# Two attention blocks: residual additions by accumulating transfers, the last pair's reciprocals spread inside VectorE, and the normed input in one ScalarE step

## The chip, the cores and the metric

The kernel runs on one core of a Trainium2 chip. The metric is the device time of that core in microseconds (us), for all eight images and both layers in one launch. A core has five engines that run their own queues in order and meet only at semaphores: TensorE (PE, matrix products), VectorE (DVE), ScalarE (ACT), GpSimd (POOL) and SyncE (SP, which here issues the transfers). Sixteen DMA engines move data between HBM and the on-chip buffer, whoever issues the transfer.

## What is computed

Eight images of 512 channels by 1024 pixels pass through two blocks of the same form: group norm, a 1x1 convolution to q, k and v, attention with 8 heads of 64 channels over the 1024 pixels, an output projection with bias, and the residual addition. Cut to what matters:

```
xg = x.reshape(B, GROUPS, -1)
xn = ((xg - mean) * rsqrt(var + EPS)).reshape(B, C, H, W)
xn = xn * norm_gamma[None, :, None, None] + norm_beta[None, :, None, None]
qkv = einsum('oc,bchw->bohw', qkv_w, xn) + qkv_b[None, :, None, None]
attn = softmax(einsum('bhds,bhdt->bhst', q, k) * scale, axis=-1)
out = einsum('bhst,bhdt->bhds', attn, v).reshape(B, C, H, W)
return x + einsum('oc,bchw->bohw', proj_w, out) + proj_b[None, :, None, None]
```

The second block has the same mathematics with separate weights wq, wk, wv, wp. Everything is float32.

## The kernel before

A job is one image in one layer: 16 jobs, numbered 0 to 15, in pairs of images (two images in layer 0, then the same two in layer 1). Two images lie in the on-chip buffer as `x` tiles of 4 channel chunks by 1024 pixels. The job's output is added into the same tile (the residual), so job n+2 reads as input what job n wrote when n is in layer 0. When n is in layer 1 the finished quarters are stored and the next image is loaded in their place.

All projections use a fast matrix-product scheme with seven products for a 2x2 block product (`ORDER`, `OUTER`, line 42 on), which trades products on TensorE for sums of blocks on VectorE. The V projection uses one level of it. The K, Q and output (O) projections use two levels: seven outer products ("chains"), each of seven inner products of 128x128 by 256 columns.

Stages, in the order in which TensorE runs them:

1. **Attention of job n** (`Attention.run`, L829): 8 groups (a pair of heads and half of the pixels) of 8 steps. In a step TensorE makes scores `sc` (L740), ScalarE makes `e = exp(sc)` (L745), VectorE adds `e` into the group's row sums `acc` (L757), and TensorE multiplies `e` with `v` into `po` (L771). At a group's end (`finish`, L776) VectorE reduces `acc` to `r` (L783) and adds the two halves of `po` into `q` (L790), which from then on holds the attention's output. After each second group four small transfers gather `r` into `lr` (L800), `invert` makes the reciprocals (L808 to L811), one transfer writes them to a DRAM scratch `rd` (L812), two transfers broadcast them from there to all partitions as `rb` (L817), and `normalise` (L823) multiplies `q` by `rb`.
2. **V phase of job n+1** (`v_phase`): 14 steps of 4 products (L443). Its results leave PSUM by ScalarE copies (L456) and VectorE additions (L458). During it VectorE makes the sums of the attention's output that the O projection needs (`out_sums`, L866: `to`, lines 337 to 343, and `os`, lines 472 to 477).
3. **Deep phases** (`deep_phases`, L512): 21 chains of 7 products (L574), O of job n, then K and Q of job n+1. Chain c+1 starts before chain c ends. Each chain fills an `epool` tile `p` with four pieces, two by ScalarE (L584, L586) and two by VectorE (L588, L590). The function `end` (L594) queues what is to be done with finished `p` tiles in a list `outer`. For O these are the residual additions, `x += p` on VectorE (`more`, L609, recorded at L603). Two of the seven products of each chain (7 and 3) take one step from the lists: `soon` (sums for later chains) and then `outer`, or, where `outer` is empty, `extra` (statistics of the next input, loads of the next image, all with a lowest chain number).

The order on each engine is written by hand. `later(delay, fn)` puts a step at a model time, `advance` moves that time while products are recorded, and `chores` puts steps at numbered steps of the attention: 64 steps in an attention. In chores lie the norm of the next input (`scale` on VectorE, L273, then `shift` on ScalarE in place, L279), its sums (L337 to L343) and, from job 3 on, half of the two-level sums (`deep_first[4:]`). The other half, and in the first jobs both, is put into the V phase and after it with `later`.

Buffers: `epool` has LEAD + 3 = 5 tiles of 4 KB per partition, shared by the `e` of the attention and the `p` of the deep phases. The weights of the chains come through a ring of RING = 8 tiles, fetched by SP 2.5 model us after a tile is used (`used`, L201). The output bias (`make_out_bias`, L906: the projection of the v bias) is made after attention 0 and attention 2 with two `epool` tiles, three loads and VectorE steps at the start of the V phase. Factors of weights for later jobs are made in the attentions 0 to 2 (`first_factors`).

Of the kernel before, what the change touches and what calls it, by code (L numbers as in the profile page):

```python
# [9 lines left out]
F32 = mybir.dt.float32  # L10
# [34 lines left out]
RING = 8  # L45
# [25 lines left out]
def fast_path(  # L71
# [13 lines left out]
    epool = ctx.enter_context(tc.tile_pool(name="epool", bufs=LEAD + 3))  # L85
# [130 lines left out]
    class Norm:  # L216


        def __init__(self, n):
            b, layer = jobs[n]  # L220
            self.n, self.b, self.layer = n, b, layer
            self.stats = small.tile([P, NC, 2, 6], F32, tag="stats", name=f"stats_{n}", bufs=1)
            self.mv = small.tile([P, NC, 2], F32, tag="mv", name=f"mv_{n}")
            self.mr = small.tile([P, NC, 2], F32, tag="mr", name=f"mr_{n}")
            self.mul = small.tile([P, NC], F32, tag="mul", name=f"mul_{n}", bufs=1)

# [39 lines left out]
        def factors(self, chunks):  # L266
            g0 = self.layer * NVEC + GAMMA
            nc.vector.tensor_mul(
                self.mul[:, chunks], self.mr[:, chunks, 1], env.vec_sb[:, g0 : g0 + NC][:, chunks]
            )  # L270

        def scale(self, cc, cols=slice(0, S)):
            nc.vector.tensor_scalar(  # L273
                xn[0][:, cc, cols], xs[self.b][:, cc, cols], self.mr[:, cc, 0:1],
                self.mul[:, cc : cc + 1], ALU.subtract, ALU.mult,
            )

        def shift(self, cc, cols=slice(0, S)):
            nc.scalar.activation(  # L279
                xn[0][:, cc, cols], xn[0][:, cc, cols], AF.Identity,  # L280
                bias=env.vec(self.layer, BETA, cc),
            )
# [24 lines left out]
    def norm_steps(n):  # L307
        norm = Norm(n)

        def scale(cc):  # L310
            if cc == 0:
                norm.factors(slice(0, NC))
                xn[0] = acts.tile([P, NC, S], F32, tag="xn", name=f"xn_{n}")
            norm.scale(cc)

        shift = norm.shift
        reads = [lambda cc=cc, sh=sh: norm.stat(cc, sh) for cc in range(NC) for sh in range(2)]
        reads.append(norm.gather)
        steps = [norm.groups]
        for cc in range(NC + 1):  # L320
            def both(cc=cc):
                if cc > 0:
                    shift(cc - 1)
                if cc < NC:
                    scale(cc)
            steps.append(both)
# [185 lines left out]
    def deep_phases(n, extra, outs=None):  # L512
# [81 lines left out]
        def end(c):  # L594
# [10 lines left out]
            if which == O:  # L605
# [3 lines left out]
                def more(oh, sh, *parts):  # L609
                    to_ = xt[:, 2 * oh : 2 * oh + 2, sh * HALF : (sh + 1) * HALF]  # L610
                    for part in parts:
                        add(to_, to_, p(part))

                def done(oh, sh):
                    if layer == 1:
                        rows = slice(oh * CH, (oh + 1) * CH)
                        cols = slice(sh * HALF, (sh + 1) * HALF)
                        last = outer.pop()
                        outer.append(lambda: (last(), nc.sync.dma_start(
                            out[b, rows, cols].rearrange("(c p) s -> p c s", p=P),  # L620
                            xt[:, 2 * oh : 2 * oh + 2, cols],
                        )))
# [3 lines left out]
                elif o == 2:  # L626
                    more(0, 0, 2)
                    done(0, 0)
                elif o == 6:
                    add(p(6), p(6), p(1))  # L630
                    more(0, 1, 6)
                elif o == 5:
                    more(0, 1, 5)
                elif o == 7:
                    add(p(7), p(7), p(6))
                    more(1, 1, 7, 5)
                    done(1, 1)
                elif o == 3:
                    more(1, 0, 7)
                    more(0, 1, 3)  # L640
                    done(0, 1)
                elif o == 4:
                    more(1, 0, 4)
                    done(1, 0)
# [75 lines left out]
    class Attention:  # L720
# [55 lines left out]
        def finish(self, g):  # L776

            n, q, m = self.n, self.q, g % 2
            hp, sh = self.groups[g]
            to_ = q[:, hp, sh * HALF : (sh + 1) * HALF]  # L780
            if m == 0:
                self.r = small.tile([P, 2, RP], F32, tag="r", name=f"r_{n}_{g}", bufs=1)
            nc.vector.tensor_reduce(  # L783
                self.r[:, m, :], self.acc.pop(g).rearrange("p j (b e) -> p (j b) e", e=RP), AX.X,
# [13 lines left out]
            lr = small.tile([RP, NQ, 2, RP], F32, tag="lr", name=f"lr_{n}_{g}", bufs=1)  # L798
            for i in range(NQ):
                nc.sync.dma_start(lr[:, i], self.r[i * RP : (i + 1) * RP])  # L800
            rd = dram.tile([2, 2, HALF], F32, tag="rd", name=f"rd_{n}_{g}")
            rb = []

            def invert():
                lt = small.tile([RP, 2, RP], F32, tag="lt", name=f"lt_{n}_{g}", bufs=1)
                ri = small.tile([RP, 2, RP], F32, tag="ri", name=f"ri_{n}_{g}", bufs=1)
                rt = small.tile([RP, 2, RP], F32, tag="rt", name=f"rt_{n}_{g}", bufs=1)
                nc.vector.tensor_reduce(lt, lr.rearrange("p a g b -> p g b a"), AX.X, ALU.add)  # L808
                nc.vector.reciprocal(ri, lt)
                for i in range(2):  # L810
                    nc.vector.transpose(rt[:, i, :], ri[:, i, :])  # L811
                nc.sync.dma_start(rd.rearrange("m j (b e) -> (j b) m e", e=RP), rt)  # L812
                nc.vector.tensor_max(lmax, lmax, lt)
                nc.vector.tensor_max(rmax, rmax, ri)
                rb.append(apool.tile([P, 2, HALF], F32, tag="rb", name=f"rb_{n}_{g}", bufs=1))
                for j in range(2):
                    nc.sync.dma_start(  # L817
                        rb[0][j * HD : (j + 1) * HD],
                        rd[:, j, :].unsqueeze(0).to_broadcast([HD, 2, HALF]),
                    )  # L820

            def normalise():
                nc.vector.tensor_mul(place, place, rb[0])  # L823

            ends = g + 1 == len(self.groups)
            later(9.9 if ends else 7.6, invert)
            later(16.4 if ends else 16.2, normalise)

# [16 lines left out]
    def judge():  # L845
        nc.vector.tensor_max(lmax, lmax, rmax)
        nc.vector.tensor_max(lmax[:, 0, :], lmax[:, 0, :], lmax[:, 1, :])
        worst = small.tile([RP, RP], F32, tag="worst", name="worst", bufs=1)
        nc.vector.tensor_copy(worst, lmax[:, 0, :])
        nc.vector.tensor_reduce(worst[:, 0:1], lmax[:, 0, :], AX.X, ALU.max)  # L850
        turned = small.tile([RP, RP], F32, tag="turned", name="turned", bufs=1)
# [14 lines left out]
    def out_sums(n, outs):  # L866
# [10 lines left out]
        steps = outs.steps(0) + [start] + outs.steps(3) + outs.steps(1) + [part(1)]  # L877
        steps += outs.steps(2) + [part(2)] + outs.steps(4) + [part(3)]
        early = 9.0 if n in (0, 2) else 3.2
        times = (0.3, 1.1, 1.9, early, early + 0.8, 15.2, 16.0, 16.8, 18.0, 18.8, 19.6, 20.8, 21.6, 22.4)  # L880
# [25 lines left out]
    def make_out_bias(layer, delay):  # L906


        rows = [
            epool.tile([P, 2, HALF], F32, tag="e", name=f"rows_{layer}_{i}") for i in range(2)  # L910
        ]
        bvb = apool.tile([P, C], F32, tag="px", name=f"bvb_{layer}")
        for i in range(2):
            nc.sync.dma_start(
                rows[i], wrows[layer][i * CH : (i + 1) * CH].rearrange("(oc p) c -> p oc c", p=P)
            )
        nc.sync.dma_start(bvb, bv[layer : layer + 1, :].to_broadcast([P, C]))

        def part(oc):
# [471 lines left out]
```

## Time and profile before

| | us |
|---|---|
| median of three runs | 3327.54 |
| lowest and highest | 3326.61, 3329.2 |
| profiled execution: run, and span from the first to the last instruction | 3330.16, 3328.4 |
| attention to attention (start of the scores), jobs 5 to 6 | 1142.26 to 1345.88: 203.6 |
| the same, jobs 1 to 2 | 301.04 to 517.23: 216.2 |
| VectorE busy, ScalarE busy | 2854.9, 1893.4 |
| GpSimd busy | 24.0 |

A line of an instruction group reads: line, engine, operation, tile written and tiles read, shapes, count, then busy time and mean duration in ns, then the time that the engine sat idle just before these instructions and what ended most of it. TensorE's busy time counts overlapping matmuls, so it is not a measure of useful work; what matters are its idle times. The stage from the end of one attention to the start of the next takes about 90 us of the 203.6, the attention about 113.

### The profile page before, as it was taken

The page shows a single profiled execution, that of the slowest core. Times are in us where ns is not written, and L with a number is a line of the kernel's source. Part 1 is how long each engine was busy: PE and PEld are TensorE (multiplying, and loading weights), DVE is VectorE, ACT ScalarE, POOL GpSimd, SP SyncE. Part 2 cuts the span into 40 slices and gives each one's busy share as a digit, 9 for nine tenths or more (in the row PEclk, how much of TensorE's full clock was granted, in tenths as well). Part 3 has the DMA queues.
Part 4 walks back from the last instruction along what each step waited for, and adds up shares of the span by engine and source line. Part 5 has one row for each costly group of instructions (what it writes and reads, how often), then busy time and mean ns, then how long its engine had stood idle before and what let it go on. Part 6 is the DMA issues. An engine that isn't in the chain of part 4 may idle for free.

```text
span 3328.4 us, 57847 instructions
## 1 busy us (share of the span) xinstructions
PE 3225.0 (97%) x22870; PEld 1854.2 (56%) x22870; DVE 2854.9 (86%) x3980; ACT 1893.4 (57%) x3026; POOL 24.0 (1%) x31
## 2 busy tenths in 40 slices
PE   9989999999999999999999999999999999999999
PEld 7356374473745737456383664836547365473743
DVE  8997988988889898888988889788897888989876
ACT  4646646456464664646646466564655646566463
POOL 0000000000000000000000000000000000000000
PEclk9999999999999999999999999999999999999999
DMA  8234142250412304124051221403315031230401
GB/s 296 69 126 115 66 140 83 68 189 15 151 59 60 100 22 121 33 71 139 22 181 30 78 76 27 135 21 103 108 37 174 15 104 56 55 106 16 144 26 47
DMA packets 143863, 289.98 MB, mean 87 GB/s; under 512 B 40040, under 2 KB 52960, under 8 KB 142560
## 3 DMA queue, kind: packets, MB, share of 16 engines
q1 hardware_dynamic: 143584, 286.22, 28.1%
q8 instruction: 181, 2.97, 0.4%
q14 instruction: 98, 0.80, 0.1%
HBM read 232.73 MB, written 51.31 MB: 85 GB/s over the span
## 4 chain that ended last, share of the span: by engine, by line
PE 72%; DVE 20%; DMA 4%; issue 2%; ACT 2%; SPq 1%; DVEq 0%; POOL 0%; ACTq 0%
PE sc L740 24%; PE po L771 22%; PE vd L574 9%; PE zd L574 8%; DVE acc L757 4%; PE yd L574 3%; PE ud L574 3%; DMA rb<-rd 2%; DVE x L603 1%; ACT e L745 1%; DVE os L472 1%; DVE v L458 1%; DVE os L473 1%; PE pp L709 1%; DVE os L476 1%
## 5 line engine op out<-in xcount | busy, mean ns | idle before, releaser
L745 ACT ACTIVATE e<-sc 128x1024 f32<-128x1024 f32 x1024 | 1043.1, 1023 | 572.9 <-PE sc L740 486.5
L740 PE MATMUL sc<-q,k 64*64 64x512 f32 x8192 | 1064.3, 591 | 20.9 <-ACT e L745 18.9
L771 PE MATMUL po<-e,v 64*64 64x512 f32 x8192 | 1058.9, 590 | 0.0
L757 DVE TENSOR_TENSOR acc<-acc,e 128x1024 f32<-128x1024 f32 x768 | 936.4, 1219 | 54.5 <-ACT e L745 6.9
L740 PEld LDWEIGHTS sc<-q,k 64*64 64x64 f32 x8192 | 308.3, 133 | 587.5 <-issue 531.1
L771 PEld LDWEIGHTS po<-e,v 64*64 64x64 f32 x8192 | 313.5, 133 | 566.4 <-issue 557.4
L574 PE MATMUL vd<-deep,w 128*128 128x256 f32 x900 | 256.6, 384 | 6.5 <-DVE p L590 6.0
L574 PE MATMUL zd<-deep,w 128*128 128x256 f32 x892 | 247.9, 380 | 0.9 <-DVE p L588 0.6
L755 DVE TENSOR_TENSOR acc<-e,e 128x1024 f32<-128x1024 f32 x128 | 156.4, 1222 | 103.0 <-ACT e L745 103.0
L574 PEld LDWEIGHTS vd<-deep,w 128*128 128x128 f32 x900 | 168.1, 190 | 49.3 <-DVE p L590 14.4
L574 PEld LDWEIGHTS zd<-deep,w 128*128 128x128 f32 x892 | 169.6, 190 | 24.5 <-DVE p L588 1.0
L603 DVE TENSOR_TENSOR x<-x,p 128x1024 f32<-128x1024 f32 x135 | 164.2, 1216 | 0.0
L783 DVE TRANSPOSE_TENSOR_REDUCE r<-acc 128x32 f32<-128x1024 f32 x128 | 158.6, 1239 | 0.6
L574 PE MATMUL vd<-os,w 128*128 128x256 f32 x420 | 126.7, 391 | 28.4 <-DVE p L588 28.4
L443 PE MATMUL z<-w,t 128*128 128x256 f32 x480 | 116.1, 391 | 24.7 <-DVE v L458 24.7
L456 ACT COPY v<-z 128x512 f32<-128x512 f32 x32 | 18.7, 586 | 180.8 <-PE z L443 180.8
L443 PEld LDWEIGHTS z<-w,t 128*128 128x128 f32 x480 | 92.8, 196 | 42.9 <-DVE v L458 30.3
L823 DVE TENSOR_TENSOR q<-q,rb 128x1024 f32<-128x1024 f32 x64 | 77.5, 1212 | 44.8 <-DMA rb<-rd 44.8
L603 DVE TENSOR_TENSOR p<-p,p 128x1024 f32<-128x1024 f32 x94 | 114.3, 1216 | 0.0
L443 PE MATMUL z<-w,xn 128*128 128x256 f32 x480 | 110.1, 383 | 0.0
L592 ACT COPY s<-zd 128x256 f32<-128x256 f32 x173 | 64.6, 373 | 77.5 <-PE zd L574 77.5
L574 PEld LDWEIGHTS vd<-os,w 128*128 128x128 f32 x420 | 79.1, 193 | 49.0 <-DVE p L588 39.2
(201 smaller groups left out, 3947.0 us busy)
## 6 DMA issues: line engine op xcount, KB each, us to landing
w<-deep SPq DMA_DIRECT2D x287, 448.0 KB
w<-keep SPq DMA_DIRECT2D x129, 256.0 KB
rb<-rd SPq DMA_DIRECT2D x128, 256.0 KB
deep<-w SPq DMA_DIRECT2D x42, 448.0 KB
x<-x_dram SPq DMA_DIRECT2D x28, 512.0 KB
out_dram<-x SPq DMA_DIRECT2D x28, 512.0 KB
keep<-raw SPq DMA_DIRECT2D x5, 1792.0 KB
lr<-r SPq DMA_DIRECT2D x256, 8.0 KB
```

The lines of the kernel that those rows point to most:

```text
L443: nc.tensor.matmul(ps[:, ti * CH : (ti + 1) * CH], r[:, cc, t0 : t0 + P], w[:, cc, :], start=(start and ti == 0 and cc == 0), stop=(cc == ...
L458: nc.vector.tensor_add(to_, tokens(ps), tokens(s5))
L574: nc.tensor.matmul(ps, lhs[:, FACTOR[i], :], moving[i], start=start, stop=True, skip_group_check=True,)
L592: return chain(product, lambda ps: nc.scalar.copy(s5, ps), put, z, y, u, w)
L603: outer.append(lambda: nc.vector.tensor_add(to_, a, b))
L740: nc.tensor.matmul(sc[h * HD : (h + 1) * HD, j, :], k[r, hp, k0 : k0 + HD], q[r, hp, sh * HALF : (sh + 1) * HALF], start=True, stop=True,)
L745: nc.scalar.activation(e, sc, AF.Exp, scale=SCALE)
L755: nc.vector.tensor_add(acc[g], self.es[i - 1], e)
L757: nc.vector.tensor_add(acc[g], acc[g], e)
L771: nc.tensor.matmul(po[g][j * HD : (j + 1) * HD, h, :], v[r, kc, d0 : d0 + HD], e[r, j, :], start=(kc == 0), stop=(kc == NT - 1),)
L783: nc.vector.tensor_reduce(self.r[:, m, :], self.acc.pop(g).rearrange("p j (b e) -> p (j b) e", e=RP), AX.X, ALU.add, apply_transpose=True,)
L823: nc.vector.tensor_mul(place, place, rb[0])
```

## The change

- **Residual additions.** `more` no longer queues a VectorE addition `x += p`. It issues a transfer on the GpSimd queue that adds `p` into the quarter of `x` (`accum_op=ALU.add`), nine per job, 512 KB each. Some are issued at the chain's end, others from the list `outer` after a VectorE sum they need. The first part of quarter (1, 0) is added at the end of outer product 7, no longer at that of outer product 3. The stores of finished quarters are put 8 model us later with `later`.
- **Last pair of an attention.** The gather of `r` becomes three VectorE copies, and the broadcast becomes three small copies and one VectorE transposition of a 128 x 1024 stretch, in place of transfers. Its steps are put at 0.0, 0.2, 2.0 and 4.0 in place of 9.9 and 16.4. The other pairs keep their way through DRAM, with three gathering transfers in place of four (the first quarter stays where it is).
- **Normed input.** `scale` and `shift` become one ScalarE step with a factor and an offset per channel, made by two more tiny VectorE operations. In the opening job two of four chunks are done by VectorE in one step.
- **Output bias.** Its loads and eight VectorE steps move from the V phase after attentions 0 and 2 to the list `extra` of the deep phases before attention 0 and before attention 2. Its buffers come from `apool`.
- **Buffers and order.** `epool` has 6 tiles and the weight ring 7. The sums for O are put earlier in the V phase. The direct two-level sums of the next input (`deep_first[:4]`) move from the V phase to `extra` in the O chains, and the others (`deep_first[4:]`) to the attention in all jobs. Statistics start at chain 15 in place of 14, loads of the next image at 11 in place of 8. The first input's statistics for job 1 move ahead of attention 0, and factors of weights start a little earlier.

The core of the diff:

```
-RING = 8
+RING = 7
...
-    epool = ctx.enter_context(tc.tile_pool(name="epool", bufs=LEAD + 3))
+    epool = ctx.enter_context(tc.tile_pool(name="epool", bufs=LEAD + 4))
...
+        def apply(self, cc, cols=slice(0, S), scalar=True):
+            to_, x, one = xn[0][:, cc, cols], xs[self.b][:, cc, cols], slice(cc, cc + 1)
+            if scalar:
+                nc.scalar.activation(
+                    to_, x, AF.Identity, bias=self.off[:, one], scale=self.mul[:, one]
+                )
...
-                def more(oh, sh, *parts):
-                    to_ = xt[:, 2 * oh : 2 * oh + 2, sh * HALF : (sh + 1) * HALF]
-                    for part in parts:
-                        add(to_, to_, p(part))
...
+                def more(oh, sh, part, ends=False):
+
+                    cols = slice(sh * HALF, (sh + 1) * HALF)
+                    to_ = xt[:, 2 * oh : 2 * oh + 2, cols]
+                    nc.gpsimd.dma_start(to_, p(part), accum_op=ALU.add)
+                    if ends and layer == 1:
                         rows = slice(oh * CH, (oh + 1) * CH)
...
+                        later(8.0, lambda: nc.sync.dma_start(
+                            out[b, rows, cols].rearrange("(c p) s -> p c s", p=P), to_
+                        ))
...
                 if o == 1:
                     more(0, 0, 1)
                 elif o == 2:
-                    more(0, 0, 2)
-                    done(0, 0)
+                    more(0, 0, 2, True)
                 elif o == 6:
                     add(p(6), p(6), p(1))
-                    more(0, 1, 6)
+                    outer.append(lambda: more(0, 1, 6))
                 elif o == 5:
-                    more(0, 1, 5)
+                    more(1, 1, 5)
+                    outer.append(lambda: more(0, 1, 5))
                 elif o == 7:
                     add(p(7), p(7), p(6))
-                    more(1, 1, 7, 5)
-                    done(1, 1)
+                    outer.append(lambda: (more(1, 1, 7, True), more(1, 0, 7)))
                 elif o == 3:
-                    more(1, 0, 7)
-                    more(0, 1, 3)
-                    done(0, 1)
+                    more(0, 1, 3, True)
                 elif o == 4:
-                    more(1, 0, 4)
-                    done(1, 0)
+                    more(1, 0, 4, True)
...
+            def spread():
+                if ends:
+                    nc.vector.transpose(
+                        box[0].rearrange("p m (b e) -> p m b e", e=RP),
+                        ri[:, :, 0, :].unsqueeze(3).to_broadcast([P, 2, RP // 2, RP]),
                     )
...
+            times = (0.0, 0.2, 2.0, 4.0) if ends else (0.0, 7.6, 7.7, 16.2)
+            for at, step in zip(times, (gather, invert, spread, normalise)):
+                later(at, step)
...
-        times = (0.3, 1.1, 1.9, early, early + 0.8, 15.2, 16.0, 16.8, 18.0, 18.8, 19.6, 20.8, 21.6, 22.4)
+        times = (0.1, 1.0, 2.5, 4.5, 5.5, 6.5, 7.5, 8.6, 14.0, 15.8, 16.5, 17.5, 19.2, 21.0)
...
-            for at, step in zip((4.8, 6.0, 8.9, 10.1, 30.0, 31.5, 33.0, 34.5), deep_first):
-                later(at, step)
...
-            extra = deque()
+            extra = deque((0, fn) for fn in deep_first[:4])
             if jobs[n][1] == 1 and jobs[n][0] + 2 < B:
-                extra.append((8, lambda b=jobs[n][0] + 2: (x_tile(b), load_x(b))))
+                extra.append((11, lambda b=jobs[n][0] + 2: (x_tile(b), load_x(b))))
...
-                extra.extend((14, fn) for fn in reads)
+                extra.extend((15, fn) for fn in reads)
```

## The prediction

> **What bounds the kernel now.** I read the page's engine line first and then the groups of TensorE with their idle times, because TensorE runs almost without a break and only its waits can be won.
>
> ```profile
> PE 3225.0 (97%) x22870; PEld 1854.2 (56%) x22870; DVE 2854.9 (86%) x3980; ACT 1893.4 (57%) x3026; POOL 24.0 (1%) x31
> ...
> L740 PE MATMUL sc<-q,k 64*64 64x512 f32 x8192 | 1064.3, 591 | 20.9 <-ACT e L745 18.9
> ...
> L574 PE MATMUL vd<-deep,w 128*128 128x256 f32 x900 | 256.6, 384 | 6.5 <-DVE p L590 6.0
> ...
> L603 DVE TENSOR_TENSOR x<-x,p 128x1024 f32<-128x1024 f32 x135 | 164.2, 1216 | 0.0
> ...
> L574 PE MATMUL vd<-os,w 128*128 128x256 f32 x420 | 126.7, 391 | 28.4 <-DVE p L588 28.4
> L443 PE MATMUL z<-w,t 128*128 128x256 f32 x480 | 116.1, 391 | 24.7 <-DVE v L458 24.7
> ...
> L823 DVE TENSOR_TENSOR q<-q,rb 128x1024 f32<-128x1024 f32 x64 | 77.5, 1212 | 44.8 <-DMA rb<-rd 44.8
> ```
>
> TensorE's own waits sum to 20.9 + 6.5 + 28.4 + 24.7 = 80.5 us, and 11.3 more before the group zd<-os (further down the list of groups): 92 us of 3328. Almost all end with VectorE (p, v) or ScalarE (e). So work taken off VectorE pays where it delays a p, v or e, and not elsewhere. Where is that? The busy times by stage of one middle job (columns: stretch, its length, busy us of PE, weight loads, DVE, ACT, POOL, granted clock, DMA share, GB/s) and the timeline of its V phase:
>
> ```profile
> 1255.30:1279.10 23.80, 22.80 (x108) 19.80 (x105) 19.34 (x32) 5.21 (x9) 0.00 (x0) 1.00 0.47 140
> 1279.10:1300.50 21.40, 19.39 (x89) 16.46 (x89) 18.46 (x35) 11.60 (x31) 0.00 (x0) 1.00 0.36 108
> 1300.50:1345.90 45.40, 45.27 (x214) 39.61 (x212) 36.11 (x58) 28.99 (x76) 0.00 (x0) 1.00 0.43 127
> 1345.90:1459.00 113.10, 112.21 (x1031) 39.79 (x1031) 101.95 (x116) 73.22 (x77) 1.40 (x1) 1.00 0.09 23
> ```
>
> ```profile
> 1274.64 1.23 DVE L823 TENSOR_TENSOR q<-q,rb 128x1024 f32<-128x1024 f32 x1 [2.71 <-DMA rb<-rd]
> ...
> 1277.32 2.00 PE L443 MATMUL z<-w,t 128*128 128x256 f32 x8 [1.00 <-DVE v L458]
> ...
> 1285.97 0.70 PE L574 MATMUL vd<-os,w 128*128 128x256 f32 x2 [1.05 <-DVE p L588]
> ```
>
> VectorE stands still for 2.71 us on the broadcast of the reciprocals, the sums of O behind it are late, and TensorE waits in the V phase and twice in the O chains (the second time at 1299.29, 0.96 us). In the K and Q chains (third row) TensorE loses nothing. The place is the O boundary.
>
> **What the Trainium skill says.** (1) "DMA: Bandwidth & Descriptors", Anatomy of one DMA: a transfer costs about 2.0 us plus its bytes at 436 GB/s, so 3.2 us for 512 KB. Here two broadcasts, 512 KB together, take 5.1 to 6.6 us in the chain of waits. So contention adds to it. (2) The same page, SWDGE vs HWDGE: accumulation goes through GpSimd alone, which makes the descriptors in software. No run here shows it yet. (3) "Collectives: The Full Stack", the bandwidth ceiling: an add in the transfer is half as fast because it reads two sources, not because adding takes time. Not shown here either. (4) "SBUF — State Buffer", Who interferes with whom: a two-input VectorE operation does not stop descriptor writing. The trace before has no such case.
>
> **The change part by part**, against the profiled span of 3328.4 (0.9 above the median run, which is less than I can resolve).
>
> *Residual additions.* 135 x 1.216 = 164.2 us leave VectorE, 10.9 per boundary, all in or just after the O chains. In return deep_first[:4], 4 x 1.22 = 4.9 us, comes from the V phase into the O chains. The second row's 18.5 us becomes about 12.5 of 21.4, and the V row loses 4.9.
>
> *Last pair.* The wait on rb<-rd (44.8 us over 14 boundaries) goes. Added per job: six small copies (no row; the 32x64 rows of L813 and L814 take 0.17 to 0.20, a 128x2 copy 0.16) about 1.0 us, and one transposition of 128x1024. No row has it: at least 0.18 (a 32x32 one, L811), at most about twice a 1024-column pass. I take 1.24, which the transposing reduction over 1024 columns takes (L783). Two 0.18 go away. Net 1.9 us more busy and about 3 less waiting, but the normalised q comes earlier: VectorE ends r 3.4 us after TensorE's last product of the attention (timeline), then copies 1.0, reduction and reciprocal 1.1, maxima 0.4, transposition 1.24, first sums 1.6, product 1.2: at about 10 us, against 20.5 now (1275.87 - 1255.4). The V phase then holds 19.3 - 4.9 + 1.9 us and O sums that were late before (about 5), so 21 of 24: no wait, and the product that waited at 1277.32 has its v about 4 us early.
>
> *Normed input.* L273 leaves (52.2 us, 3.2 per attention). ScalarE's count stays at 60 full pieces of 1.10 us, and it no longer waits for L273 (46.5 us). The attention's slip (0.68 us of idle at 1196.8, where e comes late) should mostly go. A sixth e tile helps the same.
>
> *Output bias.* Its eight steps (0.68 each, 5.5 us a time) and a 4.5 us wait for loads leave the V phases after attentions 0 and 2, where TensorE loses most (216.2 us for that job against 203.6). They come back in chains before attentions 0 and 2, with weight preparation there: I charge 3 us.
>
> *Two-level sums to the attention in jobs 0 to 2*: 3.8 us of VectorE, against 3.2 freed. Nothing, since the stage has about 11 us of slack (fourth row). Ring of 7: TensorE uses a weight tile every 7 x 0.43 = 3.0 us, so six ahead are 18 us of cover against a few us of landing: nothing. SP gains: 448 small transfers for reciprocals become 288. It gets later stores, behind which weights queue; the 18 us cover these.
>
> *Sum.* Each wait also costs the refilling: the pair after a wait takes 0.70 us for 0.43 (above), so 0.27 x about 85 waits = 23 us beside the 92. I take nearly all of z<-w,t (25 of 28), three quarters of vd<-os (27 of 36), 8 of zd<-os (the rest waits for prepared weights), 15 of 26 in the scores, nothing of vd<-deep: 75. Less 3 for the bias: 72.
>
> *What the transfers may give back.* A p tile is free only when its transfer has landed. With 0.43 us a product, counted from the start of O: the tile of chain 5 is wanted again by chain 11, whose first piece is written after 81 products, at 34.8. The quarter (0, 1) takes three transfers, each waiting for the one before. The first needs the VectorE sum after chain 2, at 24 x 0.43 + 1.2 = 11.5. So they fit if 3T < 23.3: T, from issue to landing, up to 7.8 us. My estimate of T: 2.0 + 2 x 1.2 = 4.4 us alone by (1) and (3). With 0.4 of the DMA engines taken by weights (DMA share above) the moving part stretches to 4 us, so 6.0, and about 0.5 for descriptors. Lower bound 3.2 (a plain copy), upper bound 10 to 11 if adding halves the rate again. At 6.5 it fits by 4 us, but eight transfers at 2.4 to 2.9 us of all 16 engines (19 to 23) and ten weights of 448 KB at 436 GB/s (10.5) make 30 to 34 us of work in a window of 30.5, so some chains will wait. I charge 1 us in each of 15 boundaries. 3328 - 72 + 15 = 3271; I say 3270.
>
> **The rivals.**
> 1. *Likeliest, 3270 (own range 3238 to 3300)*: as above. For it: every large wait names VectorE, and the K and Q chains show that VectorE at 80% leaves no wait.
> 2. *Half of the relief: 3308.* The waits come from bursts (two sums and an addition in one slot), not from the load. Sums for O and deep_first now share chains 0 to 3. Then z<-w,t goes (25), little else (10), less the 15. Against it: the slots that hold an addition today lose it.
> 3. *Slower: 3355 and above.* The accumulating transfer takes T = 10 us. Then quarter (0, 1) is done at 11.5 + 30 = 41.5, chain 11 waits 6.7 us behind ScalarE's first write, TensorE behind that, 15 times: 3256 + 100 = 3356. At T = 11, 3401. It decides from 11.5 + 3T = 34.8 + 72/15, T = 9.4 us. For it: no row prices accumulation, and the DMA engines already work at 0.36 to 0.47 in these stages. Against it: source (3).
> 4. *No change*: T near 9.4, between the two.
>
> That the change misses its aim is ruled out: the built order of the changed kernel has 135 transfers x<-p on GpSimd and no addition x<-x,p.
>
> **How the numbers follow.** Likeliest 0.52; half 0.18; slower 0.25; no change 0.05. A measurement of this kernel tells about 0.2%, 6.7 us, from no change: faster 0.70, same 0.05, slower 0.25. About 0.06 lies below 3236, and about 0.13 above 3360, so the range is 3236 to 3360.
>
> **What would show it.** VectorE busy near 2855 - 164 - 52 + 30 = 2670. Idle before z<-w,t under 3 us and before vd<-os under 10. The wait on rb gone at the boundaries. The groups ACT p (L584, L586 before) with no long idle ended by a DMA: if a row names the x<-p transfer there, or the statistics wait for it, rival 3 is at work. If the waits on p stay with no DMA in them, it is rival 2. A transposition far above 2.5 us would make the V phase wait again.

## The result and the profile after

The changed kernel takes 3369.55 us (median of four runs, 3366.25 to 3372.11) against 3328.37 beside it (3326.61 to 3330.59): ratio 1.0123, 95% interval 1.0105 to 1.014. It is 1.2% slower. Forecast were 3270 and a gain of 1.7%; the time lies above the range.

From the page of the changed kernel: the engine line, the DMA queue that GpSimd issues on (packets, MB, share of 16 engines' span), groups in the form explained above, and the issues of x<-p (count, size, median us from issue to landing).

```profile
PE 3248.1 (97%) x22870; PEld 1872.5 (56%) x22870; DVE 2701.4 (80%) x3895; ACT 1889.1 (56%) x3022; POOL 189.3 (6%) x166
...
q0 software_dynamic: 36720, 70.79, 12.2%
...
L723 PE MATMUL sc<-q,k 64*64 64x512 f32 x8192 | 1062.7, 590 | 4.5 <-ACT e L728 2.3
...
L565 PE MATMUL zd<-deep,w 128*128 128x256 f32 x892 | 264.5, 400 | 73.6 <-ACT yd L381 69.2
...
L565 PE MATMUL vd<-deep,w 128*128 128x256 f32 x900 | 265.1, 395 | 15.4 <-ACT yd L381 11.4
...
L565 PE MATMUL vd<-os,w 128*128 128x256 f32 x420 | 119.2, 381 | 2.0 <-DVE p L581 1.3
L434 PE MATMUL z<-w,t 128*128 128x256 f32 x480 | 111.0, 380 | 0.0
...
x<-p POOLq DMA_DIRECT2D x135, 512.0 KB, 8.5
```

Everything that the change was to relieve is relieved. The idle time before vd<-os falls from 28.4 to 2.0 us, before z<-w,t from 24.7 to 0.0, before the scores from 20.9 to 4.5. In its place stands a wait that was not there: 73.6 us before zd<-deep and 15.4 before vd<-deep, in chains where TensorE lost 7.4 us in all before (0.9 and 6.5). The engine named is ScalarE (yd), which only copies. What ScalarE itself waits for stands in the waits of the changed kernel (engine, tile and line that waited, what for, us in all, count, longest):

```profile
POOL x L604 <- DMA x<-p: 160.0, 36, 8.8
DVE p L579 <- DMA x<-p: 77.9, 17, 5.8
DVE p L581 <- DMA x<-p: 73.9, 23, 5.1
ACT p L575 <- DMA x<-p: 71.6, 26, 5.5
ACT p L577 <- DMA x<-p: 67.3, 25, 4.8
```

ScalarE stands 139 us (71.6 + 67.3) at the first piece of a `p` tile, and a transfer x<-p has not yet emptied that tile. The copies of `yd` that TensorE needs are queued behind. GpSimd stands 160 us because the transfer before it into the same quarter has not landed. One boundary shows how this comes about. It is the boundary before attention 6, called job 6 below: the O chains of job 5, which begin at 1279.5, then the K and Q chains of job 6. Selected lines from the timeline of the changed kernel (start, us, engine, line, operation, then idle time before and what ended it):

```profile
1286.44 1.20 POOL L604 DMA_DIRECT2D x<-p  x1 [117.07 <-ACT p L575]
1293.15 1.20 POOL L604 DMA_DIRECT2D x<-p  x1 [5.51 <-ACT yd L381]
...
1294.27 1.22 DVE L594 TENSOR_TENSOR p<-p,p 128x1024 f32<-128x1024 f32 x1
...
1295.79 2.43 POOL L604 DMA_DIRECT2D x<-p  x2 [1.44 <-DVE p L594]
1304.84 1.20 POOL L604 DMA_DIRECT2D x<-p  x1 [6.62 <-DMA x<-p]
1309.34 2.43 POOL L604 DMA_DIRECT2D x<-p  x2 [3.30 <-DMA x<-p]
1313.76 0.37 ACT L575 COPY p<-yd 128x256 f32<-128x256 f32 x1 [3.37 <-DMA x<-p]
1314.29 1.20 POOL L604 DMA_DIRECT2D x<-p  x1 [2.51 <-DVE p L579]
1314.46 0.70 PE L565 MATMUL zd<-deep,w 128*128 128x256 f32 x2 [2.42 <-ACT yd L381]
1320.55 0.47 ACT L577 ACTIVATE p<-yd,vec_sb 128x256 f32<-128x256 f32 x1 [4.28 <-DMA x<-p]
1321.35 1.46 PE L565 MATMUL zd<-deep,w 128*128 128x256 f32 x4 [1.91 <-ACT yd L381]
1324.22 0.37 ACT L575 COPY p<-yd 128x256 f32<-128x256 f32 x1 [0.91 <-DMA x<-p]
```

With chains counted from 0, the six `p` tiles go round, so chain 9 needs the tile of chain 3. That tile is read by two transfers, and the second of them is the second into quarter (0, 1). It could be issued only at 1304.84, when the first, issued at 1295.79, had landed (9.0 us), and landed itself at 1313.76 (8.9 us). ScalarE waits 3.37 us for it, then 4.28 for the tile of chain 4 (issued at about 1310.5, free at 1320.55: 10.0 us) and 0.91 for that of chain 5 (1314.29 to 1324.22: 9.9 us). TensorE loses 2.42 and 1.91 us. Around these two waits, in windows of the changed kernel (stretch, length, busy us of PE, weight loads, DVE, ACT, POOL, granted clock, DMA share, GB/s):

```profile
1311.80:1315.20 3.40, 0.98 (x5) 0.68 (x4) 1.42 (x2) 0.95 (x4) 0.92 (x1) 1.00 1.08 283
1315.20:1318.60 3.40, 3.40 (x9) 2.70 (x8) 0.47 (x2) 0.72 (x2) 0.28 (x1) 0.50 1.14 210
1318.60:1322.00 3.40, 1.49 (x7) 0.99 (x6) 1.44 (x2) 1.05 (x3) 0.99 (x1) 1.00 1.07 248
1322.00:1325.40 3.40, 3.40 (x10) 2.69 (x9) 0.57 (x2) 1.56 (x4) 0.21 (x1) 0.50 1.01 170
```

Two things are to be seen. The DMA share is at or above 1.0, so all sixteen engines are taken throughout. And after each of these two waits TensorE runs a 3.4 us stretch at half its clock (0.50), which costs another 1.7 us each. Over the whole execution the mean clock is 0.989, before 0.996: 37 and 13 us of full clock lost (3364.5 x 0.011, 3328.4 x 0.004).

By stage, beside the rows shown of before:

```profile
1257.00:1279.50 22.50, 22.50 (x108) 19.86 (x106) 21.91 (x43) 5.21 (x9) 0.00 (x0) 1.00 0.35 108
1279.50:1300.80 21.30, 21.30 (x100) 18.81 (x99) 15.51 (x28) 13.11 (x34) 4.83 (x4) 1.00 0.76 186
1300.80:1352.00 51.20, 46.73 (x203) 39.64 (x205) 28.28 (x48) 27.29 (x72) 6.03 (x5) 0.93 0.74 183
1352.00:1464.10 112.10, 111.89 (x1031) 39.94 (x1031) 100.07 (x116) 73.47 (x77) 1.42 (x1) 1.00 0.08 21
```

The V phase is 1.3 us shorter and the O chains have no gap, but the K and Q chains (third row) take 51.2 us where they took 45.4. The loss is made in the O chains, where the transfers are issued, and paid 20 us later. In nine of the other boundaries TensorE has one long wait of 2.75 to 4.00 us there, with a stretch at half clock at its end, where job 6 has two shorter ones.

### The profile page after: what moved, and what is told of

Same layout as the page of the kernel before. It is cut to its first block, busy times and chain, and to the rows that moved or that the text cites. A ratio compares the mean times of both kernels' runs of the same rounds, so it can differ in the third digit from the quotient of the medians.

```text
span 3364.5 us, 57800 instructions
## 1 busy us (share of the span) xinstructions
PE 3248.1 (97%) x22870; PEld 1872.5 (56%) x22870; DVE 2701.4 (80%) x3895; ACT 1889.1 (56%) x3022; POOL 189.3 (6%) x166
## 3 DMA queue, kind: packets, MB, share of 16 engines
q0 software_dynamic: 36720, 70.79, 12.2%
## 5 line engine op out<-in xcount | busy, mean ns | idle before, releaser
L565 PE MATMUL zd<-deep,w 128*128 128x256 f32 x892 | 264.5, 400 | 73.6 <-ACT yd L381 69.2
L604 POOL DMA_DIRECT2D x<-p x135 | 163.3, 1311 | 2114.3 <-ACT p L575 1523.4
L565 PE MATMUL vd<-deep,w 128*128 128x256 f32 x900 | 265.1, 395 | 15.4 <-ACT yd L381 11.4
L579 DVE TENSOR_TENSOR p<-vd,s 128x256 f32<-128x256 f32 x63 | 26.6, 423 | 135.8 <-DMA x<-p 73.7
L565 PE MATMUL vd<-os,w 128*128 128x256 f32 x420 | 119.2, 381 | 2.0 <-DVE p L581 1.3
L385 ACT COPY ud<-vd 128x256 f32<-128x256 f32 x173 | 61.8, 357 | 79.1 <-PE vd L565 58.1
L434 PEld LDWEIGHTS z<-w,xn 128*128 128x128 f32 x480 | 90.2, 190 | 23.6 <-issue 12.2
L385 ACT COPY ud<-zd 128x256 f32<-128x256 f32 x156 | 55.7, 357 | 82.0 <-PE zd L565 81.0
```

The costliest lines, as they stand in the source:

```text
L385: nc.scalar.copy(u, z)
L434: nc.tensor.matmul(ps[:, ti * CH : (ti + 1) * CH], r[:, cc, t0 : t0 + P], w[:, cc, :], start=(start and ti == 0 and cc == 0), stop=(cc == ...
L565: nc.tensor.matmul(ps, lhs[:, FACTOR[i], :], moving[i], start=start, stop=True, skip_group_check=True,)
L604: nc.gpsimd.dma_start(to_, p(part), accum_op=ALU.add)
```

## The experiments

The expectations use letters. A is the theory that the transfers lose more than the rest of the change wins, through tiles that come free late. Within it, A1 lays this on the time and order of the transfers themselves, A2 on DMA engines that are full, C1 on the adding, as against C2, the queue's order, the making of descriptors or the crowd of weights. The rivals are that another part of the change is at fault (B; in the run with a seventh tile B' is crowding or late weights), or that VectorE's relief was never there.

A simple measure beside the times is the length of job 6's deep phases in the trace, from the first O product to the next attention's first score: 66.7 us before, 72.4 after.

### Additions back on VectorE, and left out

```diff
 e1_adds_on_vector, against the changed kernel
-                    nc.gpsimd.dma_start(to_, p(part), accum_op=ALU.add)
+                        add(to_, to_, p(part))
... (places in the chains, stores and deep_first[:4] as before)

 e2_no_adds, against the changed kernel
-                    nc.gpsimd.dma_start(to_, p(part), accum_op=ALU.add)
```

> The changed kernel with the residual additions back on VectorE (and the direct two-level sums back in the V phase, since the O chains have no free slots for them then). Theory A (the accumulating transfers land late, hold the p tiles, and that alone makes the change slow; all else in it gains): 3255 to 3285 us, no wait of ScalarE or VectorE on x<-p, scores and V phase as in the changed kernel within 2 us per job, one or two short waits on p in the O chains. Theory B (the new order of the sums, the smaller weight ring or the moved two-level sums cost the time): 3330 or more, with TensorE still losing 5 us or more per job in the K chains.

> The changed kernel with the nine residual transfers left out (x is then never added to, so this part of the computation is missing). A: 3235 to 3255, TensorE loses under 2 us per job in the deep phases from job 4 on and its clock is never halved there. B: above 3330.

Measured: e1 3280.01 us, ratio 0.9841 (0.9824 to 0.9857), as A expects. e2, which leaves out the residual addition, 3231.21, ratio 0.9692 (0.9673 to 0.9711), 4 us below A's range. The deep phases of job 6 take 67.1 and 64.2 us.

So the whole of the loss lies in the transfers. All other parts together win 1.6%. Taking the additions off VectorE at no cost would win another 1.5% (0.9841 to 0.9692, about 50 us; e1 also has the direct two-level sums in their old place, which is not taken apart here). Carrying them as transfers costs 4.3% (0.9692 to 1.0123): 138 us between the two medians. e1 also shows what VectorE's additions still cost once all else is changed (groups of e1):

```profile
L565 PE MATMUL vd<-os,w 128*128 128x256 f32 x420 | 124.3, 389 | 18.9 <-DVE p L579 17.3 <-DVE p L581 1.5
...
L565 PE MATMUL zd<-os,w 128*128 128x256 f32 x300 | 89.0, 386 | 19.5 <-DVE p L581 19.5
```

38.4 us of idle time stay there, which in the changed kernel are 2.0 and 0.0. In e2 the waits in the other chains are gone (groups of e2):

```profile
L565 PE MATMUL vd<-deep,w 128*128 128x256 f32 x900 | 256.6, 384 | 4.9 <-DVE p L581 4.4 <-DVE p L579 0.5
...
L565 PE MATMUL zd<-deep,w 128*128 128x256 f32 x892 | 248.9, 381 | 4.2 <-DVE p L579 3.7 <-DVE p L581 0.2
```

### A copy in place of an addition

```diff
 e3_plain_copy, against the changed kernel
-                    nc.gpsimd.dma_start(to_, p(part), accum_op=ALU.add)
+                    nc.gpsimd.dma_start(to_, p(part))
```

> The changed kernel with the nine transfers per job as plain copies on the same GpSimd queue, with the same waits (x is overwritten, not added to: the addition is missing). C1 (the transfer is slow because adding reads two sources): landing falls from 8.5 us to 5 to 6, the waits on x<-p in the K chains go almost entirely, 3245 to 3265. C2 (it is slow through the queue's order, descriptor making or the crowd of weights): landing stays at 7.5 or more and the time above 3320.

Measured: 3237.02 us, ratio 0.9709 (0.969 to 0.9729), 8 us below the range of C1. The kernel leaves the addition out and keeps every transfer, wait and byte, and is within 6 us of no transfers at all. From its page, the GpSimd queue and the landing of a transfer:

```profile
q0 software_dynamic: 19440, 70.79, 6.0%
...
x<-p POOLq DMA_DIRECT2D x135, 512.0 KB, 5.6
```

The bytes are the same 70.79 MB, the engines' time is half (6.0% of the span against 12.2%), and the packets are 19440 against 36720. 12.2% of 3364.5 us over 135 is 3.0 us of all sixteen engines for one accumulating transfer, 6.0% of 3235.2 is 1.44 for a copy. C1 holds: neither GpSimd's queue nor transfers as such cost much, but adding does. What makes the adding dear, a second read or the smaller packets, this run doesn't take apart.

### Fewer transfers

```diff
 e4_five_transfers, against the changed kernel
-                    outer.append(lambda: more(0, 1, 6))
+                    outer.append(lambda: more(0, 1, 6, by_dma=False))
-                    more(1, 1, 5)
-                    outer.append(lambda: more(0, 1, 5))
+                    outer.append(lambda: more(1, 1, 5, by_dma=False))
+                    outer.append(lambda: more(0, 1, 5, by_dma=False))
-                    outer.append(lambda: (more(1, 1, 7, True), more(1, 0, 7)))
+                    outer.append(lambda: more(1, 1, 7, True))
+                    outer.append(lambda: more(1, 0, 7, by_dma=False))
... (by_dma=False: nc.vector.tensor_add(to_, to_, p(part)); the last two
     transfers are issued from the list outer)

 e7_six_transfers, against e4
-                    outer.append(lambda: more(1, 0, 7, by_dma=False))
+                    outer.append(lambda: more(1, 0, 7))
```

> The changed kernel with five of the nine additions per job as transfers (both of quarter (0,0) and the last of each other quarter but (1,0)'s first and the first two of (0,1), the first of (1,1) on VectorE). A: no transfer waits for another's landing except the second of (0,0), each lands before its p tile is wanted: 3245 to 3270, at or below e1. B: 3340 or more.

> The kernel of five transfers with a sixth, the first addition into quarter (1,0), put on the transfer queue beside that into (1,1). A: the last transfer of (1,0) now waits for its first, and lands at about 22 + 8 + 8 = 38 us after the start of O, where its tile is wanted at 38 to 40: 3245 to 3262, within 0.3% of the five. More than 3275 if a second same-quarter pair in the queue is already too many.

Measured: five transfers 3252.49 us, ratio 0.9753 (0.9737 to 0.977), the best complete kernel here and 2.5% faster than the one before. Six: 3281.24, ratio 0.9842 (0.9826 to 0.9859). That misses the main expectation and falls under the other one, that a second pair of transfers into one quarter is already too many. With 0, 5, 6 and 9 transfers the times are 3231, 3252, 3281 and 3370 us. From none to five, with four additions back on VectorE as well, it is 21 us. The sixth costs 29, though it takes an addition off VectorE, and each of the last three 29 on average. So there is no one price per transfer. e4 from its page:

```profile
q0 software_dynamic: 20400, 39.33, 7.4%
...
L565 PE MATMUL vd<-os,w 128*128 128x256 f32 x420 | 122.4, 384 | 14.7 <-DVE p L579 12.6 <-DVE p L581 1.9
...
x<-p POOLq DMA_DIRECT2D x75, 512.0 KB, 7.3
```

and the waits of e7:

```profile
ACT p L577 <- DMA x<-p: 31.6, 16, 4.2
...
DVE p L581 <- DMA x<-p: 31.2, 12, 4.5
```

In e4 neither ScalarE nor VectorE waits for x<-p at all, and VectorE's additions leave 14.7 us before vd<-os. In e7 one transfer more brings the wait for the tile back. The timelines of the two show how. In e4 the last transfer of a boundary is issued 26.2 us after the start of O (jobs 3 to 14). In e7 the sixth is issued right behind two others, and three at 3.0 us of all engines each need 9 us. The last transfer, into the same quarter as the sixth, must wait until that has landed, and goes out at 33.8 to 35.8. Over 39 us of a boundary, from 6.5 us after the start of O, the share of the DMA engines is about the same in both, 0.87 to 0.94 in e4 and 0.88 to 0.94 in e7 (seven boundaries each), and 1.02 to 1.03 in the changed kernel. So the sixth transfer is dear because another must wait for it behind a burst, and not because the boundary as a whole is fuller than with five.

### A seventh tile, and the weight ring that pays for it

```diff
 e5_seventh_tile, against the changed kernel
-RING = 7
+RING = 5
-    epool = ctx.enter_context(tc.tile_pool(name="epool", bufs=LEAD + 4))
+    epool = ctx.enter_context(tc.tile_pool(name="epool", bufs=LEAD + 5))

 e9_ring_of_five, against the changed kernel
-RING = 7
+RING = 5
```

> The changed kernel with a seventh epool tile (and the weight ring cut from 7 to 5 to make room). A (a p tile is wanted again before its transfer has landed): every tile is wanted one chain, 3.0 us, later, so each of the two or three waits per boundary shrinks by up to that and most clock halvings go: 3270 to 3320. If the transfers' mere crowding of the DMA engines were the cost, or weights came late (B'), it stays at 3360 or gets worse, with waits on w<-deep.

> The control for the seventh tile: the changed kernel with the weight ring cut from 7 to 5 and nothing else, so that the run with the seventh tile differs from it by the tile alone. A: slower than that run (3418.75 us) by 20 to 70 us, with waits on x<-p as long as in the changed kernel (about 140 us each on ScalarE and VectorE, against 41 there) and waits on w<-deep beside them. If the tile does nothing: equal to it within 5 us.

Measured: e5 3418.75 us, ratio 1.0255 (1.0235 to 1.0276); e9 3421.75, ratio 1.0272 (1.0252 to 1.0293). Theory A missed both times. The other branch came true in both: e5 gets worse, with waits on w<-deep, and e9 lies within 5 us of it. First the waits of e9, then those of e5:

```profile
PE vd L565 <- DMA w<-deep: 68.3, 20, 6.4
...
ACT p L577 <- DMA x<-p: 33.6, 10, 5.2
...
ACT p L575 <- DMA x<-p: 27.4, 14, 3.7
```

```profile
PE vd L565 <- DMA w<-deep: 68.8, 20, 6.2
...
ACT p L575 <- DMA x<-p: 40.9, 7, 6.4
```

Against e9, the seventh tile takes ScalarE's waits for x<-p from 61 to 43 us, but the time only from 3421.75 to 3418.75, and the two runs of each overlap. The shorter ring makes TensorE wait some 68 us for weights, 8.5 in the changed kernel. So beside a ring of 5 one tile more gains nothing that can be seen. Whether it would help beside a ring of 7, where TensorE waits little for weights, stays open: no run here has both.

### Lighter weights

```diff
 e12_lighter_weights, against the changed kernel
-            nc.sync.dma_start(w, deep[which, layer, o])
+            nc.sync.dma_start(w[:, :4], deep[which, layer, o][:, :4])
-                    ps, lhs[:, FACTOR[i], :], moving[i], start=start, stop=True,
+                    ps, lhs[:, FACTOR[i] % 4, :], moving[i], start=start, stop=True,
```

> The changed kernel with the loads of the chains' weights cut from seven blocks to four (448 to 256 KB each); products that need blocks 4 to 6 use blocks 0 to 2 in their place, so TensorE does the same work on wrong weights. The nine accumulating transfers, their waits, tiles and order stay. Theory A2 (the sixteen DMA engines are full in this stretch: nine transfers of 3.0 us and thirteen weight loads of 1.2 us, 42 us of work in about 39): the work falls by about 6 us to 36, landing falls from 8.5 to about 7, the waits of ScalarE on x<-p fall from 139 us to under 50, and the time to 3270 to 3315. Theory A1 (each transfer is slow by itself, by its descriptors, its completion and its order in the queue): landing stays above 8, time within 15 us of the changed kernel's 3370.

The chains' weights become 256 KB in place of 448, and three of the seven products use another product's weights. With these wrong numbers the kernel's own guard on the sums sends it, after the fast path, through its general path as well, and the whole takes 9700.99 us. Only the fast path can be compared. Its last projection (L692) starts at 3282.4 us, that of the changed kernel at 3331.1: 48.7 us earlier, so about 3316 to the end. The waits in the fast path of this kernel:

```profile
ACT p L577 <- DMA x<-p: 59.7, 22, 4.8
...
ACT p L575 <- DMA x<-p: 24.9, 16, 5.9
```

84.6 us against 139. Of the accumulating transfers and their order nothing was changed, only other traffic beside them, and they land in 7.3 us in place of 8.5. So A2 has its direction: full engines are part of the cause. A third of the loss of 138 us goes; 2.4 us of it are shorter waits of TensorE for weights (8.5 to 6.1). The waits on x<-p fell less than A2 expected (under 50 us), and the time lies at the edge of its range. That fits with e7, where the order of the transfers, each waiting for the one before into its quarter, costs time by itself. How the 138 us divide between order and load, no run here tells.

### The parts in the kernel before

Each part put alone into the kernel before. The diffs are those of the change, cut to the part:

```diff
 e6_transfers_alone, against the kernel before
-                        add(to_, to_, p(part))
+                    nc.gpsimd.dma_start(to_, p(part), accum_op=ALU.add)

 e8_spread_alone, against the kernel before
-            later(9.9 if ends else 7.6, invert)
-            later(16.4 if ends else 16.2, normalise)
+            times = (0.0, 0.2, 2.0, 4.0) if ends else (0.0, 7.6, 7.7, 16.2)
... (with gather, invert and spread of the change)

 e10_normed_alone, against the kernel before
-            norm.scale(cc, cols)
-            norm.shift(cc, cols)
+            norm.apply(cc, cols, cc % 2 == 1)
... (with the factor, the offset and the one ScalarE step of the change)

 e11_bias_elsewhere_alone, against the kernel before
-                later(0.3, lambda layer=jobs[n][1]: make_out_bias(layer, 3.2))
+                load, bias_steps = make_out_bias(1)
+                extra.append((8, load))
+                extra.extend((11, fn) for fn in bias_steps)
```

> The kernel before with only the residual additions changed: nine accumulating transfers per job, stores 8 us later, 5 epool tiles, everything else as it was. A: every tile is wanted 3.0 us earlier than in the changed kernel, so the K chains wait about 3 us more per boundary, while the V phase and the scores keep their old waits: 3400 to 3470. If the slow part of the change were another one: below 3335.

> The kernel before with only the last pair's reciprocals gathered and spread by VectorE, sums of O at their old times. A's ledger: the wait of 44.8 us of VectorE on the broadcast goes and the V phase's 29 us of TensorE loss mostly with it, plus a part of the loss on vd<-os: 3285 to 3305. If the wait on the broadcast was slack (rival): within 5 us of before.

> The kernel before with only the normed input made in one ScalarE step. A's ledger: the idle time of the scores (20.9 us) falls by about half or more and nothing else changes: 3312 to 3322 beside 3328 to 3334 of before. If ScalarE's own step was the cause of the late e: no change.

> The kernel before with only the output bias made in the K and Q chains before attentions 0 and 2. A's ledger: the V phases after attentions 0 and 2 lose 6 us less in all, their O chains 8 to 12 less, the K and Q chains with weight preparation 3 to 6 more: 8 to 15 us faster than before. Rival: the steps only change place: within 5 us.

| alone | us | ratio (95% interval) |
|---|---|---|
| transfers that add, five tiles | 3462.38 | 1.0386 (1.0366 to 1.0407) |
| reciprocals of the last pair by VectorE | 3298.87 | 0.9898 (0.9882 to 0.9915) |
| normed input in one step | 3302.18 | 0.9916 (0.9899 to 0.9932) |
| output bias elsewhere | 3327.88 | 0.9993 (0.9984 to 1.0001) |

The transfers alone cost 3.9%, and the spread wins 1.0%, both within their expected ranges. The spread, its ring of 8 unchanged, takes the wait before z<-w,t from 24.7 to 7.4 us, as its groups show:

```profile
L574 PE MATMUL vd<-os,w 128*128 128x256 f32 x420 | 125.7, 387 | 21.4 <-DVE p L588 21.4
L443 PE MATMUL z<-w,t 128*128 128x256 f32 x480 | 112.7, 383 | 7.4 <-DVE v L458 7.4
```

The one ScalarE step does another thing. In e10 the idle time before the scores falls from 20.9 to 2.3 us, and z<-w,t stays at 23.2:

```profile
L731 PE MATMUL sc<-q,k 64*64 64x512 f32 x8192 | 1062.0, 590 | 2.3 <-ACT e L736 0.2
```

It was worth 28.8 us against the kernel before beside it, and at 3302.18 lies 10 us under its expected range.

The move of the bias wins where it was to win, and gives it back. From first product to first product, the V phase after attention 0 shrinks from 29.8 to 24.0 us and that after attention 2 from 25.2 to 22.6, but attention 2 grows from 117.0 to 121.2. The total does not move, so the rival expectation (within 5 us) holds.

## Why the prediction was wrong

**The relief** (72 us): right in kind, too small. Without any additions (e2) the kernel is 3.08% faster, 103 us. The waits went as forecast: before z<-w,t under 3 us (0.0), before vd<-os under 10 (2.0). What was missed shows when the times from one product's start to the next, beyond the usual (0.216 us for 256 columns, 0.107 for a score), are added up: the V phases lost 34 us before and 5 in e2, the deep phases 68 and 21, the attentions 42 and 20. That is 29 + 47 + 22 = 98 of the 103, where I had taken 25 + 35 + 15. Part of it is clock, which I had not counted: its mean is 0.999 in place of 0.996, 10 us. VectorE came to 2701 us, against the 2670 forecast.

**The spread**: right. From the groups of the changed kernel, the transposition, the product after it and the one-step norm (the norm with its two shapes kept apart):

```profile
L831 DVE TENSOR_TENSOR q<-q,rb 128x1024 f32<-128x1024 f32 x64 | 77.5, 1211 | 0.0
...
L277 ACT ACTIVATE xn<-x,off,mul 128x1024 f32<-128x1024 f32 x60 | 74.1, 1236 | 4.2 <-DVE off L272 4.2
...
L825 DVE STREAM_TRANSPOSE rb<-ri 128x1024 f32<-128x1024 f32 x16 | 19.6, 1226 | 0.0
```

The transposition takes 1.226 us, taken as 1.24. The product with `rb` ends at 1267.8, 10.9 us after the V phase's first product (about 10 forecast), and its idle time for the broadcast, 44.8 before, is 0.0. The one ScalarE step takes 1.24 us over 1024 columns, where the old shift took 1.15; the prediction's 1.10 is the mean over both shapes of the old shift. Nothing came of the difference.

**The output bias** (3 us charged, its gain counted in the relief): alone it leaves the total where it was (e11, 0.9984 to 1.0001).

**"What the transfers may give back"**: here the prediction failed. "I charge 1 us in each of 15 boundaries" stood against 138 us, 9.2 per boundary. Four terms:

1. *The start.* Quarter (0, 1) was to start at 11.5 us after the start of O and starts at 16.3. Chains are interleaved, so the tile of chain 2 is written at about 12.7 and not at 10.3. Then the VectorE sum it needs stands 2.1 us behind the sums for `os` in its own queue, to begin at 1294.27.
2. *T.* Estimated at 6.5 (0.5 of it for descriptors, for which the prediction had no measurement), it is 6.7 for the first transfer of the boundary (1286.44 to 1293.15, where the second waited for it) but 9.0, 8.9 and 9.9 for the three of quarter (0, 1). They end at 1324.2, 44.7 us after the start of O, where the estimate said 11.5 + 19.5 = 31.0. Of the 13.7 us, 4.8 are the late start, 8.3 the three transfers (27.8 against 19.5), and 0.6 the pauses between them. By the prediction's count the tile was wanted at 34.8.
3. *The engines.* The sum of 30 to 34 us of work in a window of 30.5 was the right warning, and the price was set beside it rather than from it. Measured, one transfer takes 3.0 us of all sixteen engines, not 2.4 to 2.9, and all nine share the stretch with the weights. In the 39 us between 1286 and 1325 GpSimd's queue takes 69.8% of the engines' time and SyncE's queue, mostly weights, 32.8%: 27.2 + 12.8 = 40 us of work. The packets are those of ten weight loads (1280, 128 to a load), as many as the prediction took; the thirteen loads and 42 us in the expectation of e12 were too many. With full engines the landing time is not a constant to put into a chain, but what is left of the engines.
4. *The clock.* After the waits of some 2 us TensorE ran 3.4 us at half clock, which the forecast did not have. 37 us of full clock were lost in the changed kernel, and 3 without the additions (e2, clock 0.999).

In sum, against e2: idle time before zd<-deep and vd<-deep 89.0 against 9.1 (80 us), clock 34, and the remaining 24 us or so of the 138, by subtraction, for refilling after waits and what else the traces don't separate.

**The rivals.** Rival 3 named the place (tiles of `epool`, ScalarE's first write, TensorE behind it), the sign that would show it, and T = 10. T was 8.5 by its median and 9 to 10 where it decides. So it had the right mechanism, at a chance of 0.25. Its deciding point of 9.4 was worked from a start at 11.5 and a relief of 72: from 16.3 and 103 it is 16.3 + 3T = 34.8 + 103/15, T = 8.5. With the measured start and landings its way of counting gives a last tile free at 44.7 and wanted at 34.8, 9.9 us late, 15 times, so 3328 - 103 + 149 = 3374 against the 3369.55 measured. That this comes so near is in part luck. Without transfers (e2) chain 11 writes its first piece 36.9 us after the start of O and not 34.8, so the tile is 7.8 late, near the 8.2 us that job 6's deep phases take more than in e2, and 15 x 7.8 is 117 us of the 138. The first tile to be late is that of chain 3, though, and not that of chain 5. Rival 2 (the bursts stay) fell: the waits on `p` sums went. Its mechanism is seen in e1, where additions on VectorE leave 38 us.

**"Collectives: The Full Stack", bandwidth ceiling** of the Trainium skill, that adding halves the rate because two sources are read, agrees in its factor: 3.0 us of the engines against 1.44 for a copy, 2.1 times. The reason that it gives no run here shows. From the fit in **"DMA: Bandwidth & Descriptors", Anatomy of one DMA**, a copy of 512 KB is estimated at 3.2 us. Here even the copies beside other traffic land after 5.6 (e3). The estimate built on that fit was right for the first transfer alone.

**"Ring of 7: nothing"** was not tested apart, by the changed kernel with a ring of 8. At 5, e9 loses 1.5% against the changed kernel (1.0272 and 1.0123), so the argument of cover, six ahead of a landing of a few us, fails at four ahead when transfers crowd the engines. At 7 the waits tell: in e1 and e2, which have a ring of 7, no engine waits for w<-deep, and in the changed kernel TensorE waits 8.9 us for it. So the ring of 7 costs nothing without the transfers and little with them.

## What to carry to other kernels

An operation moved from a busy engine to the DMA engines is paid there in engine time: add up all transfers of the stretch, the ones that are already there too, and if the sum comes near the stretch's length, take landing times as unknown and move only as much as leaves room (here five additions of nine, which beats both kernels). Count too which transfers must wait for one another: here the sixth transfer delayed the last one by 8 to 10 us in each boundary, and cost 29 us in all. When a buffer is freed by a transfer, follow it to the engine that writes the buffer next and to what is queued behind that write. Take a change of several parts apart: here two parts win 1.0% and 0.8% alone, one nothing, and one loses more than all the others win.

## What the runs showed of the hardware

- In an accumulating transfer from one on-chip buffer to another, packets are 2048 B and take 178 ns each (median), while those of 2048 B on SyncE's queue take 84 ns. The plain copy of the same tiles goes as packets of 4096 B at 164 ns.
- GpSimd is busy 1.2 us for each accumulating transfer that it issues and 0.7 us for each copy (timelines of the changed kernel and of e3), 163.3 us in all in the changed kernel.
- TensorE's granted clock falls to 0.50 for about 3.4 us after single waits of about 2 us (job 6: 1.91 and 2.42 us), but not after every one: in e1 a wait of 2.10 us that ends at 658.15 is followed by none. In the changed kernel this shows as a mean of 0.989, and 0.999 where the waits are gone (e2).
- A VectorE transposition over 128x1024 takes 1.226 us, about as long as a product of that size (1.211).
